# The last turns of a two-layer graph attention kernel: an order of their own, and late steps on other engines

## The chip, the cores and the metric

The kernel runs on one core of one Trainium2 chip. The metric is the device time of one execution in microseconds (us). It was taken in three runs: 3034.12, 3035.43 and 3037.57 us, with a median of 3035.43 us. One further execution was recorded by the hardware profiler, and all times of single instructions come from it.

The engines are named as the profile names them. PE is the matrix engine and PEld its loading of weights. DVE is the vector engine, ACT the scalar (activation) engine, POOL the GpSimd engine, and SP the engine that issues the transfers. Each engine works through its own instructions in the order in which the program issues them.

## What is computed

There are 128 graphs of 128 nodes with 512 features, and an adjacency matrix for each. Two layers follow each other, each of the form `x = x + layer(relu(layernorm(x)))`.

```python
# layer 0, 8 heads of 64
m = embs @ map_w.T + map_b
n = sem / norm                              # m, split into heads, at unit length
cos_adj = (n @ n.T masked) > 0.1
p_attn = softmax(q @ k.T / 8, masked) * keep
adj = cos_adj * p_attn
out = relu(((adj @ sem_h) @ gcn_W.T) / (adj.sum(-1) + 1))
# layer 1, 4 heads of 64
attn = softmax(q @ k.T / 8, masked by adjacency)
return x + ((attn @ v) @ Wo + bo)
```

All is in float32.

## The kernel before

**Blocks and turns.** The 128 graphs are cut into 64 blocks of two graphs (`g` = 0 and 1, each 128 nodes on the 128 partitions). A block is an object of the class `Block` (L224); each of its methods is one *step*, which issues a few instructions. The tuple `TURN` (L910) lists 139 entries `(back, step, arguments)`. The loop at L1155 runs turns from -2 to 67. In a turn it goes through the list and runs each step for block `turn - back`, if there is such a block. So a block is spread over some eight turns: loading at back -3, projections of layer 0 at back 0, its attention at back 1, the end of layer 0 and the projections of layer 1 at back 2, the scores of layer 1 at back 3, and the output at back 4. The order of each engine's instructions is the order of this list. It is written out by hand (`tc.manual_schedule()`, L1071), and the list is the same for all turns. In the last turns 63 to 67 the steps of blocks that don't exist drop out, and the rest stays in the order of `TURN`.

**The steps of a block**, in the order of its life, with the engine that does the work:

- `p qk i`, `p ms i` (L378, PE): the seven products of a 2x2 Strassen scheme for queries and keys, and for `m` with the layer's second map. The banks are called X, Y and Z. `r`, `u`, `c` (L442 to L493, DVE, ACT, POOL) combine and drain them. Product 7 adds to bank Y after `u 1` has read it, product 4 after `u 2`, product 3 adds to Z after `c 1 1`.
- `squares` (ACT), `norms` (DVE), `unit` (L511, POOL): rows of `m` at unit length. For a block in the middle, 32x32 pieces are then transposed on the DVE and moved through DRAM: `nT`, `nT_put`, `nT_get`, `nT_out`. The first and the last block are `alone` (L230); for them PE transposes (L543) and ACT copies.
- `scores0` (PE), `scores0_out`, `max0` (DVE), `exps0` (ACT); `near` (PE), `near_out` (L632, DVE): scores, softmax numerators, and the cosine test. `near_T`, `near_put`, `near_get`, `near_T_out`: the transpose of this tile through DRAM, or by PE for a block that is `alone`.
- `mix0` (PE), `mix0_out` (L702, DVE), `residual` (L722, POOL), `stats1` (DVE), `rstd` (L329, POOL), `norm1` (ACT): layer 0 ends and layer 1 begins.
- `h1`, `h1_put`, `h1_get`, `h1_out` (L736 to L757): the transpose of the normed rows, through DRAM, or by PE for the last two blocks (`late`, L228). `halves` (L360, POOL): four sums of quarters for the Strassen products.
- `p qk1`, `p v` (PE) with their `r`, `u`, `c`; `scores1` (PE), `scores1_out` (L775, DVE), `exps1` (L808, ACT), `weights1` (L820, DVE, one reciprocal), `scale1` (L824, POOL, two instructions).
- `attn_T` (DVE), `attn_put`, `attn_get` (SP, four writes and a read): the transpose of the weights through DRAM. For the last block alone (`last`, L229) PE transposes and ACT copies (L855 to L863).
- `mix1` (PE), `mix1_out` (L881, ACT), `project` (L886, PE), `project_out` (L899, DVE), `store` (L904, SP). `bias1` (L732, POOL) adds the output bias to the residual beforehand.

**What is shared.** All PSUM tiles come from one pool of eight banks (L58 to L61), which are given out in turn: a product that asks for a bank waits until the readers of the bank handed out eight requests earlier are done. Most tiles in SBUF have one buffer (`keep1`), so a block's step waits for the previous block's last reader. `x1`, the residual rows, has three buffers and is loaded by `reload` (L249).

Of the kernel before, what the change touches and what calls it, by code (L numbers as in the profile page):

```python
# [10 lines left out]
AF = mybir.ActivationFunctionType  # L11
ALU = mybir.AluOpType
# [3 lines left out]
P = 128  # L16
# [4 lines left out]
def kernel(  # L21
# [21 lines left out]
    nc = tc.nc  # L43
    B, S, D = x.shape
# [6 lines left out]
    IC = INNER // P  # L51
    G = 2
    T = G * S
    NB = B // G
# [128 lines left out]
    squares = ctx.enter_context(tc.tile_pool(name="squares", bufs=2))  # L183
# [40 lines left out]
    class Block:  # L224
        def __init__(self, b):
            self.b = b

            self.late = b >= NB - 2  # L228
            self.last = b == NB - 1  # L229
            self.alone = b == 0 or self.last  # L230
            self.f = {}

        def cols(self, g):
# [125 lines left out]

        def halves(self, layer):  # L360
            A = self.quarters(layer)
            tag = f"halves{layer}"
            t = keep1.tile([P, 4, 2, S], F32, tag=tag, name=f"{tag}_{self.b}")
            S1, S2, S3, S4 = (t[:, i] for i in range(4))
            nc.gpsimd.tensor_tensor(S1, A[1][0], A[1][1], ALU.add)  # L365
            nc.gpsimd.tensor_tensor(S2, S1, A[0][0], ALU.subtract)
            nc.gpsimd.tensor_tensor(S3, A[0][0], A[1][0], ALU.subtract)
            nc.gpsimd.tensor_tensor(S4, A[0][1], S2, ALU.subtract)
            self.f["S", layer] = (S1, S2, S3, S4)

        def parts(self, kind, nm):
# [6 lines left out]
        def p(self, kind, i):  # L378
            layer = int(kind in ("qk1", "v"))
            A = self.quarters(layer)  # L380
            S = self.f.get(("S", layer))
# [339 lines left out]

        def residual(self, g):  # L722
            x1 = self.x1[:, g, :]
            nc.gpsimd.tensor_add(x1, x1, self.f["mix", g])  # L724

        def stats1(self, g):
            self.f["st", 1, g] = stats(self.x1[:, g, :], f"1_{self.b}_{g}")
# [32 lines left out]

        def scores1(self):
            f = self.f
            f["ps1"] = self.by_square(f"ps1_{self.b}", "c q" if self.last else "q c")
            for g in range(G):
                cols = self.cols(g)
                self.pairs(
                    f["ps1"],
                    g,
                    lambda r, p: f["q1"][r, p, cols],
                    lambda r, p: f["k1"][r, p, cols],  # L770
                    IC,
                    G,
                )

        def scores1_out(self):  # L775
            b, f = self.b, self.f
            pp = f["ps1"]
            if self.last:
                flat = keep1.tile([P, 2, IC, G, Q, SQ], F32, tag="s1", name=f"s1_{b}")
                f["s1_flat"] = flat  # L780
                s = flat.rearrange("p r c g q j -> p q r c g j")
            else:
                s = keep1.tile([P, Q, 2, IC, G, SQ], F32, tag="s1", name=f"s1_{b}")
            mx = small.tile([P, 2, IC, G], F32, tag="mx1", bufs=2, name=f"mx1_{b}")
            neg = self.neg1.rearrange("p q g j -> p q (g j)")
            for par in range(2):
                if self.last:
                    for c in range(IC):
                        nc.vector.tensor_add(  # L789
                            s[:, :, par, c].rearrange("p q g j -> p g q j"),  # L790
                            pp[par][:, :, c * G : (c + 1) * G].rearrange("p q g j -> p g q j"),
                            self.neg1.rearrange("p q g j -> p g q j"),
                        )
                    row = flat[:, par].rearrange("p c g q j -> p (c g) q j")
                else:
                    nc.vector.tensor_add(
                        s[:, :, par].rearrange("p q c g j -> p q c (g j)"),
                        pp[par].rearrange("p q (c g) j -> p q c (g j)", g=G),
                        neg[:, :, None, :].broadcast_to([P, Q, IC, G * SQ]),
                    )  # L800
                    row = s[:, :, par].rearrange("p q c g j -> p (c g) q j")
                nc.vector.tensor_reduce(  # L802
                    mx[:, par].rearrange("p c g -> p (c g)"), row, AX.XY, ALU.max, negate=True
                )
            f["s1"], f["mx1"] = s, mx
            f["z1"] = small.tile([P, 2, IC, G], F32, tag="z1", bufs=2, name=f"z1_{b}")

        def exps1(self, g):  # L808
            s, mx, z = (self.f[k] for k in ("s1", "mx1", "z1"))
            for par in range(2):  # L810
                for c in range(IC):
                    nc.scalar.activation(  # L812
                        s[:, :, par, c, g, :],
                        s[:, :, par, c, g, :],
                        AF.Exp,
                        bias=mx[:, par, c, g : g + 1],
                        accum_out=z[:, par, c, g : g + 1],
                    )

        def weights1(self):  # L820
            s, z = self.f["s1"], self.f["z1"]
            nc.vector.reciprocal(z, z)  # L822

        def scale1(self):  # L824
            s, z = self.f["s1"], self.f["z1"]
            for par in range(2):
                if self.last:
                    t = self.f["s1_flat"][:, par].rearrange("p c g q j -> p (c g) (q j)")
                    zz = z[:, par].rearrange("p c g -> p (c g)")[:, :, None]
                    nc.gpsimd.tensor_tensor(t, t, zz.broadcast_to([P, IC * G, S]), ALU.mult)  # L830
                    continue
                nc.gpsimd.tensor_tensor(  # L832
                    s[:, :, par].rearrange("p q c g j -> p q (c g) j"),
                    s[:, :, par].rearrange("p q c g j -> p q (c g) j"),
                    z[:, par].rearrange("p c g -> p (c g)")[:, None, :, None].broadcast_to(
                        [P, Q, IC * G, SQ]
                    ),
                    ALU.mult,
                )

        def attn_T(self):
            if self.last:
                return
            s = self.f["s1"].rearrange("p q r c g j -> p (q r c g j)")
            nc.vector.transpose(s, s)

        def attn_put(self):
            if self.last:
                return
            s = self.f["s1"].rearrange("p q r c g j -> p q (r c g j)")  # L850
            self.f["attn_dram"] = put(s, "attn", f"attn_{self.b}")

        def attn_get(self):
            t = keep1.tile([P, Q, 2 * IC * G * SQ], F32, tag="aT", name=f"aT_{self.b}")
            if self.last:  # L855
                src = self.f["s1_flat"].rearrange("p r c g q j -> p (r c g q j)")
                t = self.flat(t)
                for i, pi in enumerate(self.transposes(src, 2 * IC * G)):
                    nc.scalar.copy(t[:, i * D : (i + 1) * D], pi)
                self.f["aT"] = t.rearrange(  # L860
                    "p (r c g a j) -> p a r c g j", r=2, c=IC, g=G, j=SQ
                )
                return  # L863
            get(self.f["attn_dram"], t)
            self.f["aT"] = t.rearrange("p a (r c g j) -> p a r c g j", r=2, c=IC, g=G)
# [14 lines left out]

        def mix1_out(self):  # L881
            oT = keep1.tile([P, G, IC, S], F32, tag="oT", name=f"oT_{self.b}")
            nc.scalar.copy(oT, self.f["po1"])  # L883
            self.f["oT"] = oT

        def project(self, g):  # L886
# [23 lines left out]
    TURN = (  # L910
        (2, "mix0", 0),
        (4, "mix1"),
        (2, "mix0", 1),
        (2, "mix0_out", 0),
        (2, "residual", 0),
        (1, "scores0", 0),
        (4, "mix1_out"),
        (1, "nT_put"),
# [130 lines left out]
        (1, "near_T_out", 1),  # L1049
    )  # L1050

    blocks = {}

    def block(b):
# [16 lines left out]
    with tc.manual_schedule():  # L1071
# [12 lines left out]
        for i in range(2):  # L1084
            t = keep3.tile([P, G, D], F32, tag="x1", name=f"wT_k{i}")
# [9 lines left out]
        t = keep1.tile([P, G, KC, S], F32, tag="h1T", name="gw0")  # L1095
        gw.append(t.rearrange("p g c s -> p (g c s)"))
        t = keep1.tile([P, Q, 2, IC, G, SQ], F32, tag="s1", name="gw1")
# [53 lines left out]
        halves = (-1, "halves", 0)  # L1151
        early = [t for t in TURN if t != halves]
        early.insert(early.index((0, "unit", 0)), halves)

        for turn in range(1 + min(t[0] for t in TURN), NB + 4):  # L1155
            for back, step, *args in early if turn < 2 else TURN:
                b = turn - back
                if 0 <= b < NB and (b, step, *args) not in done:
                    getattr(block(b), step)(*args)
                    if later and turn >= 0 and step in ("u", "c") and args[0] == "ms":  # L1160
                        one_piece()
            blocks.pop(turn - 4, None)


# [44 lines left out]
```

## Time and profile before

| | |
|---|---|
| median of three runs | 3035.43 us |
| the profiled execution, its own time | 3033.84 us |
| its span, from the first to the last instruction | 3032.0 us |
| mean granted clock of PE | 0.996 |
| PE busy | 2990.2 us (99%) |
| DVE busy | 2410.0 us (79%) |
| POOL busy | 1768.7 us (58%) |
| ACT busy | 1471.3 us (49%) |
| one turn in the middle (PE's `mix1` of one turn to that of the next) | 45.7 us |

The profiled execution took 1.84 us more than its span, and 1.6 us less than the median of the three runs. A turn is read off the timeline of PE: the products of `mix1` start at 2621.59, 2667.30 and 2713.01 us. The stretch of 45.7 us from 2711.5 us on has PE busy in all of it, with DVE at 37.5, POOL at 27.6 and ACT at 22.8 us.

Turn 63, the last in which a block runs its projections of layer 0, starts on PE at 2894.85 us with `mix0` of block 61. A line of the timeline has the start, the duration, the engine, the line of the kernel, what is written and read, how many instructions are merged, and in brackets how long the engine was idle before and which instruction ended that.

### The profile page before, as it was taken

To read this page: it belongs to the slowest core of one execution; us is meant where nothing else is said; L and a number is where in the kernel's file an instruction comes from. 1 tells how busy PE (TensorE), PEld (TensorE's weight loads), DVE (VectorE), ACT (ScalarE), POOL (GpSimd) and SP (SyncE) were. 2 spreads that over 40 slices of the span, in tenths; PEclk is the share of its full clock that TensorE was granted. 3 is DMA by queue.
4 is the path that set the end of the run, shared out by engine and by line. 5 is a ranking of instruction groups with operands and counts; after the bars stand their busy time and mean duration, and the time that the engine had idled before them with its cause. 6 is when DMAs were issued, how large, how long until landed. Compare 5 with 4: busy or idle time off the path is not lost. (4 is left out here: it accounts for less than half of the span.)

```text
span 3032.0 us, 68538 instructions
## 1 busy us (share of the span) xinstructions
PE 2990.2 (99%) x25328; PEld 2372.9 (78%) x25328; DVE 2410.0 (79%) x4563; ACT 1471.3 (49%) x4637; POOL 1768.7 (58%) x2439
## 2 busy tenths in 40 slices
PE   8999999999999999999999999999999999999996
PEld 5788788787787787787787787787787787787775
DVE  3788888888888888888888888888888888888873
ACT  2454454554554554554554554554554554544542
POOL 1566566566566566566566566566565565565552
PEclk9999999999999999999999999999999999999998
DMA  4356556555556555565565565565465465465441
GB/s 155 109 159 185 175 166 182 171 172 182 166 177 182 160 183 182 156 188 177 156 191 177 156 188 182 152 191 181 149 194 179 149 192 181 149 189 181 147 140 56
DMA packets 304830, 508.39 MB, mean 168 GB/s; under 512 B 49264, under 2 KB 181104, under 8 KB 296560
## 3 DMA queue, kind: packets, MB, share of 16 engines
q1 hardware_dynamic: 301792, 503.44, 54.5%
q8 instruction: 201, 3.29, 0.4%
q10 hardware_dynamic: 2704, 0.57, 0.1%
q14 instruction: 133, 1.09, 0.1%
HBM read 273.72 MB, written 230.16 MB: 166 GB/s over the span
## 5 line engine op out<-in xcount | busy, mean ns | idle before, releaser
L617 ACT ACTIVATE s<-s,mx 128x128 f32<-128x128 f32 x1024 | 396.3, 393 | 74.1 <-DVE mx L603 74.1
L513 POOL TENSOR_TENSOR rn<-rn,mhalf 128x8 f32<-128x8 f32 x128 | 213.1, 1665 | 330.6 <-DVE rn L508 258.5
L407 PEld LDWEIGHTS py_qk<-halves,w_qk 128*128 128x128 f32 x3072 | 370.4, 193 | 41.4 <-issue 31.8
L407 PE MATMUL py_qk<-halves,w_qk 128*128 128x128 f32 x3072 | 389.2, 277 | 10.5 <-DVE k L476 6.7
L407 PEld LDWEIGHTS pz_qk<-halves,w_qk 128*128 128x128 f32 x3072 | 369.0, 192 | 28.7 <-issue 28.7
L407 PE MATMUL pz_qk<-halves,w_qk 128*128 128x128 f32 x3072 | 385.7, 275 | 0.0
L407 PEld LDWEIGHTS px_qk<-hT,w_qk 128*128 128x128 f32 x2048 | 244.0, 192 | 39.9 <-issue 32.4
L365 POOL TENSOR_TENSOR halves<-h1T 128x256 f32<-128x256 f32 x64 | 46.6, 728 | 387.9 <-ACT h1T L319 381.0
L812 ACT ACTIVATE s<-s,mx 128x128 f32<-128x128 f32 x512 | 199.2, 390 | 142.7 <-DVE mx L802 142.7
L407 PE MATMUL px_qk<-hT,w_qk 128*128 128x128 f32 x2048 | 256.8, 279 | 3.5 <-DVE mix L713 3.5
L395 PE MATMUL px_ms<-w_ms,hT 128*128 128x512 f32 x512 | 247.2, 605 | 0.0
L890 PE MATMUL py<-w_o,oT 128*128 128x512 f32 x512 | 240.7, 594 | 1.4 <-ACT oT L883 1.4
L395 PE MATMUL py_ms<-w_ms,halves 128*128 128x512 f32 x512 | 240.7, 592 | 0.0
L395 PE MATMUL pz_ms<-w_ms,halves 128*128 128x512 f32 x512 | 240.6, 592 | 0.0
L319 ACT ACTIVATE hT<-mv 128x1024 f32<-128x1024 f32 x64 | 67.6, 1057 | 318.1 <-PE py_ms L395 318.1
L724 POOL TENSOR_TENSOR x<-x,mix 128x512 f32<-128x512 f32 x128 | 162.6, 1271 | 89.5 <-DVE mix L713 57.3
L456 ACT ACTIVATE r_qk<-px_qk,b_k 128x128 f32<-128x128 f32 x256 | 73.2, 368 | 275.6 <-PE px_qk L407 271.2
L617 ACT ACTIVATION_READ_ACCUMULATOR s<-s,mx 128x1 f32 x1024 | 196.6, 192 | 0.0
L395 PEld LDWEIGHTS pz_ms<-w_ms,halves 128*128 128x128 f32 x512 | 97.3, 190 | 122.5 <-issue 107.6
L832 POOL TENSOR_TENSOR s<-s,z 128x512 f32<-128x512 f32 x126 | 128.5, 1041 | 106.0 <-DVE z L822 106.0
L395 PEld LDWEIGHTS px_ms<-w_ms,hT 128*128 128x128 f32 x512 | 92.0, 189 | 99.5 <-issue 91.8
L641 DVE SCALAR_TENSOR_TENSOR s<-pc,s 128x512 f32<-128x512 f32 x256 | 163.6, 680 | 3.3 <-PE pc L557 3.1
(140 smaller groups left out, 7121.8 us busy)
## 6 DMA issues: line engine op xcount, KB each, us to landing
d_h<-hn SPq DMA_DIRECT2D x504, 128.0 KB, 3.7
mv<-d_h SPq DMA_DIRECT2D x126, 512.0 KB, 4.4
d_near<-s SPq DMA_DIRECT2D x248, 256.0 KB, 3.8
near_mv<-d_near SPq DMA_DIRECT2D x62, 1024.0 KB, 5.4
xt<-in_x SPq DMA_DIRECT2D x64, 512.0 KB, 7.3
x<-in_x SPq DMA_DIRECT2D x64, 512.0 KB, 6.3
out<-x SPq DMA_DIRECT2D x128, 256.0 KB, 2.3
d_attn<-s SPq DMA_DIRECT2D x252, 128.0 KB, 2.4
```

The costliest lines, as they stand in the source:

```text
L319: nc.scalar.activation(t.rearrange("p g c (a j) -> p (g c) a j", a=Q), self.f.pop((key, "moved")).rearrange("p a r j -> p r a j"), func,)
L365: nc.gpsimd.tensor_tensor(S1, A[1][0], A[1][1], ALU.add)
L395: nc.tensor.matmul(bank[:, : rhs.shape[1]], lhsT=src[:, c, :], rhs=rhs, start=(first and c == 0), stop=(c == 1), skip_group_check=True,)
L407: nc.tensor.matmul(bank[:, oc * P : (oc + 1) * P], lhsT=(w_qk1 if layer else w_qk)[:, w, c, oc * P : (oc + 1) * P], rhs=src[:, c, :], star ...
L456: nc.scalar.activation(r[:, cols], X[:, cols], AF.Identity, bias=b_k[:, oc : oc + 1])
L513: nc.gpsimd.tensor_tensor(rn, rn, mhalf[:, :H0], ALU.pow)
L617: nc.scalar.activation(s[:, :, g, par, c, :], s[:, :, g, par, c, :], AF.Exp, bias=mx[:, i : i + 1], accum_out=z[:, h : h + 1],)
L641: nc.vector.scalar_tensor_tensor(sp, cp, 0.1, sp, ALU.is_gt, ALU.mult,)
L724: nc.gpsimd.tensor_add(x1, x1, self.f["mix", g])
L812: nc.scalar.activation(s[:, :, par, c, g, :], s[:, :, par, c, g, :], AF.Exp, bias=mx[:, par, c, g : g + 1], accum_out=z[:, par, c, g : g + 1],
L832: nc.gpsimd.tensor_tensor(s[:, :, par].rearrange("p q c g j -> p q (c g) j"), s[:, :, par].rearrange("p q c g j -> p q (c g) j"), z[:, par ...
L890: nc.tensor.matmul(py, lhsT=self.f["oT"][:, g, c, :], rhs=w_o1[:, c, :], start=(c == 0), stop=(c == IC - 1),)
```

## The change

A second list, `TAIL`, takes the place of turns 63 to 67. In it `back` counts from 64, so that 1 is block 63, 2 is block 62, and so on to 5 for block 59. It holds the same steps as `TURN` gives for these turns; left out are only steps that do nothing for the last blocks. Their order is new, and it isn't one turn after another: the products of blocks 61, 62 and 63 are mixed.

For the two `late` blocks (62 and 63) some steps change engine or form:

- `residual` and `halves` of layer 1 go from POOL to DVE.
- Block 62 gets what only block 63 had: rows of scores in the order that PE can transpose, eight transposes on PE, and no way through DRAM for the attention.
- `exps1` takes one parity of heads instead of one graph, and scales it at once: four exponentials on ACT, then a reciprocal and one multiplication on DVE. `weights1` and `scale1` are empty for these blocks.
- Of the two copies of the transposed attention the second goes to DVE; `mix1_out` is split into a half on ACT and a half on DVE.

```diff
-            self.last = b == NB - 1
-            self.alone = b == 0 or self.last
+            self.alone = b == 0 or b == NB - 1
...
+            add = (nc.vector if self.late and layer else nc.gpsimd).tensor_tensor
...
+            add(S1, A[1][0], A[1][1], ALU.add)
+            add(S2, S1, A[0][0], ALU.subtract)
+            add(S3, A[0][0], A[1][0], ALU.subtract)
+            add(S4, A[0][1], S2, ALU.subtract)
...
-            nc.gpsimd.tensor_add(x1, x1, self.f["mix", g])
+            (nc.vector if self.late else nc.gpsimd).tensor_add(x1, x1, self.f["mix", g])
...
-            f["ps1"] = self.by_square(f"ps1_{self.b}", "c q" if self.last else "q c")
+            f["ps1"] = self.by_square(f"ps1_{self.b}", "c q" if self.late else "q c")
...
+        def exps_last(self, par):
+            s, mx, z = (self.f[k] for k in ("s1_flat", "mx1", "z1"))
+            for c in range(IC):
+                for g in range(G):
+                    nc.scalar.activation(
+                        s[:, par, c, g],
+                        s[:, par, c, g],
+                        AF.Exp,
+                        bias=mx[:, par, c, g : g + 1],
+                        accum_out=z[:, par, c, g : g + 1],
+                    )
+            nc.vector.reciprocal(z[:, par], z[:, par])
+            t = s[:, par].rearrange("p c g q j -> p (c g) (q j)")
+            zz = z[:, par].rearrange("p c g -> p (c g)")[:, :, None]
+            nc.vector.tensor_tensor(t, t, zz.broadcast_to([P, IC * G, S]), ALU.mult)
...
-                    nc.scalar.copy(t[:, i * D : (i + 1) * D], pi)
+                    copy = nc.vector.tensor_copy if i else nc.scalar.copy
+                    copy(t[:, i * D : (i + 1) * D], pi)
...
-            nc.scalar.copy(oT, self.f["po1"])
+            if self.late:
+                nc.scalar.copy(oT[:, 0], self.f["po1"][:, 0])
+                nc.vector.tensor_copy(oT[:, 1], self.f["po1"][:, 1])
+            else:
+                nc.scalar.copy(oT, self.f["po1"])
...
-        for turn in range(1 + min(t[0] for t in TURN), NB + 4):
+        for turn in range(1 + min(t[0] for t in TURN), NB - 1):
...
+        for back, step, *args in TAIL:
+            getattr(block(NB - back), step)(*args)
```

The new list, with its entries written side by side and cut to the parts that the prediction speaks of (a number is `back`):

```text
3 mix0 0, 3 mix0 1, 3 mix0_out 0, 5 mix1, 3 residual 0, 2 scores0 1, 3 mix0_out 1, 3 stats1 0, 3 residual 1
...
2 max0 1, 5 store 0, 3 norm1 1, 3 h1, 2 exps0 0 0, 1 p qk 5, 1 c qk 0 0, 3 h1_put
...
1 p qk 3, 3 h1_get, 1 r qk 2, 2 near_out 0, 2 near_out 1, 3 h1_out, 1 p ms 1, 1 p ms 6, 3 halves 1,
1 c qk 1 0, 1 c qk 0 1, 1 p ms 5, 3 p v 1, 2 near_T 0, 2 near_T 1
...
2 mix0 0, 3 c v 1 1, 4 attn_put, 2 mix0_out 0, 3 p v 3, 3 c v 0 1, 2 mix0 1, 1 unit 1, 2 residual 0,
2 mix0_out 1, 1 scores0 0, 2 stats1 0, 2 residual 1, 2 stats1 1, 2 rstd 1 0, 2 rstd 1 1, 2 norm1 0,
4 attn_get, 1 nT_out, 1 scores0_out 0, 2 norm1 1, 1 scores0 1, 4 mix1, 4 mix1_out, 3 scores1, 1 max0 0,
1 scores0_out 1, 1 exps0 0 0, 2 h1_out, 1 near 0, 3 scores1_out, 4 project 1, 4 project_out 1, 4 project 0,
1 exps0 0 1, 3 exps1 0, 1 near_out 0, 3 exps1 1, 2 halves 1, 1 near_T_out 0, 4 project_out 0, 1 near 1
...
3 scale1, 1 reload, 3 attn_T, 2 r qk1 1, 2 p qk1 2, 3 attn_put, 2 u qk1 1, 2 p v 7
...
2 p v 3, 1 mix0 1, 2 c qk1 0 1, 1 residual 0, 3 attn_get, 3 mix1, 1 stats1 0, 2 c v 0 1, 1 mix0_out 1,
3 mix1_out, 1 residual 1, 1 rstd 1 0, 1 stats1 1, 1 norm1 0, 2 scores1, 3 project 1, 3 project_out 1,
1 rstd 1 1, 1 norm1 1, 1 bias1 1, 3 project 0, 2 scores1_out, 1 h1_out, 1 halves 1, 3 store 1,
1 p qk1 1, 1 r qk1 1, 1 p qk1 5, 1 p v 6, 1 p qk1 6, 3 project_out 0, 1 u qk1 1, 2 exps1 0, 1 p v 1, 1 p qk1 7
...
2 bias1 1, 1 c qk1 1 0, 1 u v 2, 1 p qk1 3, 1 p v 4, 2 exps1 1, 1 c v 1 0, 1 p v 5, 1 c qk1 0 1, 1 c qk1 0 0,
2 attn_get, 1 masks1, 1 scores1, 1 scores1_out, 2 mix1, 2 mix1_out, 2 bias1 0, 1 p v 2, 1 c v 1 1, 2 project 0,
1 exps1 0, 1 p v 3, 2 project_out 0, 2 store 0, 1 c v 0 0, 1 c v 0 1, 1 exps1 1, 2 project 1, 1 attn_get,
3 store 0, 1 mix1, 2 project_out 1, 2 store 1, 1 mix1_out, 1 project 1, 1 bias1 0, 1 project 0,
1 project_out 1, 1 store 1, 1 project_out 0, 1 store 0
```

## The prediction

> **What bounds the kernel now.** I read the page first. PE is 99% busy and its row is at 9 in all but the first and the last slice, so only what shortens PE's row counts, and only the tail is changed.
>
> ```profile
> PE   8999999999999999999999999999999999999996
> ...
> PEclk9999999999999999999999999999999999999998
> ```
>
> The last slice has both faults: PE not full, and its clock lowered. The table of windows from turn 63 to the end shows where (columns: us, busy us and instructions of each engine, granted PE clock, DMA share, GB/s).
>
> ```profile
> core 0: us, PE busy (x) PEld busy (x) DVE busy (x) ACT busy (x) POOL busy (x), PEclk, DMA share, GB/s
> 2895.00:2940.50 45.50, 45.50 (x392) 36.27 (x390) 34.92 (x66) 20.03 (x69) 25.25 (x32) 1.00 0.47 140
> 2940.50:2963.00 22.50, 18.54 (x210) 15.08 (x208) 16.61 (x36) 15.20 (x59) 10.84 (x16) 0.92 0.06 24
> 2963.00:2985.00 22.00, 18.90 (x180) 16.30 (x180) 10.15 (x29) 3.42 (x8) 6.40 (x10) 0.84 0.26 72
> 2985.00:3005.00 20.00, 13.86 (x108) 12.96 (x108) 7.98 (x17) 6.79 (x24) 9.56 (x13) 0.91 0.26 81
> 3005.00:3032.00 27.00, 13.44 (x62) 7.13 (x57) 5.47 (x11) 5.64 (x20) 2.04 (x2) 0.83 0.10 39
> ```
>
> Turn 63 is full. From 2940.56 us on PE waits. Its timeline has nine waits, 21.70 us together; these four are 17.42 of them:
>
> ```profile
> 2954.60 2.08 PE L557 MATMUL pc<-nT 64*128 64x128 f32 x16 [3.49 <-ACT nT L547]
> ...
> 2966.09 2.05 PE L407 MATMUL py_qk<-halves,w_qk 128*128 128x128 f32 x8 [3.44 <-DVE k L476]
> ...
> 2995.49 2.04 PE L407 MATMUL py_qk<-halves,w_qk 128*128 128x128 f32 x8 [3.29 <-DVE k L476]
> ...
> 3017.93 2.12 PE L297 MATMUL pt<-ident,s 128*128 128x128 f32 x8 [7.20 <-POOL s L830]
> ```
>
> The group behind each takes double time: eight `py_qk` products need 0.89 us elsewhere and 1.84 here (to the next group's start), with a granted clock of 0.50 in two-microsecond windows. Against full-clock groups the excess is 1.7 us behind the first, 2.7, 1.7 and 2.9 behind the others: 9.0 us. So from PE's start of turn 63 (2894.85, t = 0 below) to the span's end, 137.15 us are: 45.7 of turn 63, 55.9 of products after it (64.9 busy less 9.0), 21.7 waiting, 9.0 slow clock, and 4.85 behind the last product (3027.15 to 3032.0).
>
> The chain of waits tells why. `k` L476 (`u qk1 1`) stands on DVE behind `attn_T`, which waits for `scale1` on POOL:
>
> ```profile
> 2991.43 0.21 DVE z L822
> 2991.65 0.07 issue
> 2991.71 2.05 POOL s L832 x2
> 2993.79 0.04 DVE s L845
> ```
>
> **Part by part.**
>
> *PE's own work.* 45.7 + 55.9 = 101.6 us stay; eight transposes for block 62 are added, 0.97 us by nT's (2948.98 to 2949.95): 102.6.
>
> *Block 62's attention.* Gone: a DVE transpose (1.25), four writes and a read on SP. From 2993.79 to the read's landing (issue 2998.85 plus the tail's median of 4.2) that way took 9.3 us; SP has nothing else queued behind it. In its place are the transposes, a 0.59 ACT copy and a DVE copy of 0.68 (PSUM source, as L902). `scores1_out` has four additions of 0.41 for two of 0.69: +0.2 on a DVE that idles half of that stretch.
>
> *Scaling.* POOL's pair is 2.04 us. DVE with both inputs in SBUF takes 0.68 for 128x512 (the weight subtractions of L1148): two of those and two reciprocals of 0.2, and the first overlaps the other parity's exponentials. For block 63 that takes about 1.2 us off the chain.
>
> *Halves, residuals.* Eight POOL instructions of 0.73 become DVE instructions of 0.41 (L1148, 128x256); four of 1.27 become 0.68. DVE gets some 8.7 us with the scaling, POOL loses 15. DVE had 40 us of work in the 91 after turn 63, so there is room on average, not everywhere: at t = 42 to 68 I find it busy throughout.
>
> *Split copy of mix1_out.* 0.59 on ACT becomes two concurrent halves of about 0.4: 0.2 us each for blocks 62 and 63.
>
> *The order.* I walked the new list by hand, each engine in order at the durations of the rows above, with bank and tile reuse. PE stays full through t = 48.9. The DRAM round trips moved into it still fit: h1 of block 61 is transposed at 16.4 (11.7 before), lands near 25 and its relu ends at 26, needed at 29.2; near of block 62 lands by 42, needed at 45.2. Then the waits, without contention / with it:
>
> 1. Transposes of block 63's `n`: PE is free at 48.9; `unit` ends on POOL at 50.0 (two powers of 1.65, four products of 0.6, from `norms` at 44): 1.2 / 1.9.
> 2. `scores1` 61 needs the bank that `scores0_out` 63 frees; DVE gets there after two `mix0_out` (1.65 each), residuals (0.68), `stats1` (0.93): 0.9 / 1.2.
> 3. `h1_out` 62, whose `norm1` stands behind nT's copies on ACT: 0.6 / 0.6.
> 4. `near_T_out` 63 waits for four exponentials of 0.38, relus of 1.2, four more, and `near_out`: 1.1 / 1.1.
> 5. `p v 3` and `mix0 1`: 0.4 / 0.4.
> 6. Block 63's products wait for its `halves`: 0.3 / 3.8.
> 7. The end: `scores1` 63 now has 5.3 us of other products behind it, `mix1` and `project` of 62 and two `p v`, against a chain of about 6. With the copies of aT (0.9) and oT (0.6): 2.2 / 2.2.
>
> Sum 6.7 / 11.2. `attn_put` 61 now follows `reload` 63 on SP, which waits for block 60's stores and moves 512 KB: 0 to 2 us, I take 1. `nT_put`, `near_put` and the other transfers keep their neighbours.
>
> *The contention* is where a rule speaks against this change. The row first: POOL's first `halves` takes 0.73 us, but 1.39 where DVE ran subtractions with two SBUF inputs (L175); a small DVE instruction of 0.23 took 0.58 and ended with POOL's.
>
> ```profile
> 45.56 1.39 POOL L365 TENSOR_TENSOR halves<-hT 128x256 f32<-128x256 f32 x1 [12.63 <-ACT hT L319]
> ```
>
> ```profile
> 2944.01 0.58 DVE L710 TENSOR_SCALAR r<-r,free 128x8 f32<-128x8 f32 x1
> ```
>
> The Trainium skill ("SBUF — State Buffer", section "SBUF: two separate sides") says that DVE and GpSimd share one pair of ports as an exclusive lock, taken by a DVE instruction with two SBUF inputs for its whole length. All 16 moved instructions have two. At `halves` 63 POOL is about to run three `bias1` (1.27 each) and `masks1` (2 x 0.69) in a row, and each DVE half can wait for one of them: 1.3 + 0.7 + 0.7 + 1.3, less overlap, 3.5. Without the rule I would take 6.7 us of waits, by it 11.2; the rows say it holds, and I take 10 because POOL need not win each time.
>
> *The clock.* "TensorE: Matmul & The Clock Gate", "What's actually happening", puts the drop after an idle window of about 3.4 us; here 3.29 was enough, while 0.74, 0.66 and 1.46 between 2984.9 and 2990.2 left it at 1.00. By either, none of the waits above (1.9 at most in one piece) costs clock: 0, bounded by 2.7 for one drop.
>
> *The last store.* Before, both additions and both stores followed the last product: 4.85. Now only one of each does: 0.69 + 0.41 issue + 2.3 landing + 0.45 = 3.9.
>
> **Sum.** 102.6 + 11 + 0 + 3.9 = 117.5 against 137.15: 19.6 us less. The span becomes 3012.4, that execution 3014.2; the median stood 1.6 above it: 3016 us.
>
> **Rivals.** *Contention or a late chain is worse than taken*: one or two waits of 3 us open again, each with 1.7 to 2.9 us of half clock: 5 to 12 us back, 3021 to 3028. For it: DVE full from 42 to 68, where every delay passes on; against: 91 us of tail with three half-idle engines. *No contention*: 6.7 + 0 waits, 24 us gained, 3011. *The order does nothing*, since block 63's chain sets the end anyway: within 6 us of 3035. Against: PE would need 25 us of waits, and block 63's `mix0` in the walk is at 71, where before it came at 82.5. *Slower*: the order breaks the full turn 63. h1 61 is 3.3 us from being late, near 62 about 3, attention 60 and 61 under 1. PE can't pass a late product, so each trip late beyond this costs its lateness plus about 2.5 of clock. To lose the 19.6 us and 6 more, the four must be some 6 us late each, trips of 14 in place of 8. The trace's put-to-landing times (medians in the tail: 2.3 to 4.1 us for writes, 3.1 to 5.4 for reads) are far from that.
>
> **Numbers.** Forecast as summed, 0.58 (3012 to 3020); no contention 0.12; worse contention 0.21; nothing 0.05; slower 0.04. A measurement can tell about 0.2% (6 us) from no change. Faster by over 0.2%: 0.91; within: 0.05; slower: 0.04. For 8 in 10 I leave out the far half of the second rival's gains and the last two cases: 3009 to 3025.
>
> **What would show it.** After 2940 us the clock row stays at 1.00; PE's waits in the tail sum to about 11 us and none exceeds 2.5; DVE `halves` at 0.41, those of block 63 stretched or spaced by POOL's `bias1`; PE waits before `pt` of the last attention under 1 us. Wrong: a PE wait over 3 us before `py_qk` of block 63 or before `mix1` of 61, or any wait before t = 48.

## The result and the profile after

The changed kernel takes 3009.97 us (median of five runs, 3009.67 to 3010.41) against 3035.43 us before (five runs, 3033.86 to 3037.57): 25.5 us less. The ratio is 0.9915, with a 95% interval of 0.9904 to 0.9926. The forecast was 3016 us with a range of 3009 to 3025; the result is 6.0 us below it, just inside the lower end. The profiled execution took 3010.06 us with a span of 3008.3. That span is only 23.7 us shorter, because turn 63 began 1.3 us later in this execution (2896.14 in place of 2894.85 us), a shift that is there from the first turns on and that the change doesn't touch.

The rows of PE and of its clock, from the page of the changed kernel:

```profile
PE   8999999999999999999999999999999999999999
...
PEclk9999999999999999999999999999999999999999
```

The last slice is now full and at full clock. The table of windows shows the same for the tail (the columns are those of the table of the kernel before):

```profile
2940.50:2963.00 22.50, 21.42 (x240) 17.28 (x240) 20.29 (x48) 14.41 (x52) 11.08 (x16) 1.00 0.23 71
2963.00:2985.00 22.00, 21.24 (x215) 17.81 (x214) 17.27 (x45) 10.14 (x36) 10.28 (x14) 1.00 0.25 85
2985.00:3005.00 20.00, 18.18 (x126) 12.40 (x124) 12.50 (x30) 6.37 (x26) 0.00 (x0) 1.00 0.14 52
```

DVE, the third busy column, is busier than before in the same stretches, and the clock is 1.00 in all of them. PE's timeline lists five waits after turn 63 where it listed nine:

```profile
2950.58 1.16 PE L557 MATMUL ps<-k,q 64*128 64x128 f32 x14 [0.97 <-ACT nT L547]
...
2979.44 1.16 PE L407 MATMUL px_qk<-h1T,w_qk 128*128 128x128 f32 x8 [0.25 <-ACT h1T L753]
2980.97 1.13 PE L407 MATMUL pz_qk<-halves,w_qk 128*128 128x128 f32 x8 [0.37 <-DVE halves L365]
...
2998.24 1.63 PE L892 MATMUL po<-aT,v 128*64 128x128 f32 x16 [0.24 <-ACT aT L879]
3000.80 3.70 PE L914 MATMUL py<-w_o,oT 128*128 128x512 f32 x8 [0.92 <-DVE oT L905]
```

They sum to 2.75 us, where before it was 21.70, and no group behind them runs at double length. So the account of the tail, from PE's start of turn 63 to the span's end, is 137.15 us before and 112.16 after (3008.3 - 2896.14): waits 18.95 less, half clock 9.0 less, the piece behind the last product 1.05 less (4.85 to 3.8), the eight new transposes 0.97 more. That would be 28.0 us; 25.0 were measured, and 3.0 us lie inside the rows of PE's products.

A part of these 3.0 us is waiting too. A row merges several products, and a wait in the middle of it doesn't show in its bracket, but it does in the rows of PEld, which loads the weights:

```profile
2946.42 0.42 PEld L296 LDWEIGHTS pt<-ident,n 128*128 128x128 f32 x4 [0.35 <-POOL n L523]
...
2984.03 0.97 PEld L407 LDWEIGHTS py_qk<-halves,w_qk 128*128 128x128 f32 x8 [0.33 <-DVE k L476]
2994.70 0.52 PEld L395 LDWEIGHTS pz_v<-w_v,halves 128*128 128x128 f32 x4 [0.88 <-DVE v L482]
2998.79 0.85 PEld L892 LDWEIGHTS po<-aT,v 128*64 128x64 f32 x14 [0.35 <-DVE aT L879]
```

By the starts of the groups around them, these four cost PE some 0.4, 0.3, 0.3 and 0.5 us, 1.5 together; the kernel before has one such wait at full clock, of 0.4 (before product 6 of block 62). So about 1.1 of the 3.0 us are waits, and 1.9 are in PE's work proper.

### The profile page after: what moved, and what is told of

The parts are those of the page before. It is cut to its first block, busy times and chain, and to the rows that moved or that the text cites. A ratio compares the mean times of both kernels' runs of the same rounds, so it can differ in the third digit from the quotient of the medians.

```text
span 3008.3 us, 68541 instructions
## 1 busy us (share of the span) xinstructions
PE 2986.0 (99%) x25336; PEld 2367.4 (79%) x25336; DVE 2418.2 (80%) x4586; ACT 1469.3 (49%) x4637; POOL 1750.9 (58%) x2423
## 3 DMA queue, kind: packets, MB, share of 16 engines
q8 instruction: 201, 3.29, 0.4%
## 4 chain that ended last, share of the span: by engine, by line
PE 97%; DVE 1%; DMA 1%; POOL 0%; issue 0%; ACT 0%; ACTq 0%; SPq 0%; DVEq 0%; POOLq 0%
PE py_qk L407 17%; PE px_qk L407 11%; PE pz_qk L407 11%; PE py_ms L395 11%; PE px_ms L395 8%; PE pz_ms L395 7%; PE py L914 7%; PE po L692 4%; PE psc L557 4%; PE pc L557 4%; PE py_v L395 3%; PE ps L557 2%; PE pz_v L395 2%; PE px_v L395 2%; PE po L892 2%; PE pw_k L132 0%
## 5 line engine op out<-in xcount | busy, mean ns | idle before, releaser
L617 ACT ACTIVATE s<-s,mx 128x128 f32<-128x128 f32 x1024 | 396.4, 393 | 73.0 <-DVE mx L603 73.0
L815 ACT ACTIVATE s<-s,mx 128x128 f32<-128x128 f32 x496 | 192.9, 390 | 136.2 <-DVE mx L802 136.2
L395 PEld LDWEIGHTS py_ms<-w_ms,halves 128*128 128x128 f32 x512 | 92.5, 190 | 92.8 <-issue 92.5
```

What stands on the lines that cost most here:

```text
L395: nc.tensor.matmul(bank[:, : rhs.shape[1]], lhsT=src[:, c, :], rhs=rhs, start=(first and c == 0), stop=(c == 1), skip_group_check=True,)
L617: nc.scalar.activation(s[:, :, g, par, c, :], s[:, :, g, par, c, :], AF.Exp, bias=mx[:, i : i + 1], accum_out=z[:, h : h + 1],)
L815: nc.scalar.activation(s[:, :, par, c, g, :], s[:, :, par, c, g, :], AF.Exp, bias=mx[:, par, c, g : g + 1], accum_out=z[:, par, c, g : g + 1],
```

## The experiments

All are compared with their own runs of the kernel before (medians 3035.03, 3035.55 and 3034.48 us in the three sets), and by their medians with the 3009.97 us of the changed kernel. That was timed in a set of its own (3035.43 us before), and the medians of the kernel before differ by up to 1.1 us between the sets: a smaller difference from the changed kernel is not shown.

**The moves in the old order.** Theory: the new order carries the gain. Rival: the moves of steps to other engines carry it.

```diff
-        for turn in range(1 + min(t[0] for t in TURN), NB - 1):
+        for turn in range(1 + min(t[0] for t in TURN), NB + 4):
...
-        for back, step, *args in TAIL:
-            getattr(block(NB - back), step)(*args)
```

> All engine and form changes of the late blocks, but the last turns in the old order of TURN. Theory (the order carries the gain): near 3030 us, a gain of 3 to 8 us. The way through DRAM of block 62's attention is gone (3.3 us of wait and 1.7 of clock), the last scaling is some 1.2 us shorter, but in the old order the vector engine now stands behind block 62's exponentials before it comes to block 63's halves, which gives 2 to 3 us back. The waits before near of block 63 (3.5) and before block 62's Strassen product 7 (3.4) stay. Rival (the moves carry it): 3018 us or less, with PE waits below 10 us in the tail.

Measured: 3035.44 us, ratio 1.0001 (0.9992 to 1.0010). The moves alone gain nothing, less than either side expected. PE's timeline of this kernel still has ten waits with 20.06 us, and three of the four largest have new releasers:

```profile
2956.49 2.08 PE L557 MATMUL pc<-nT 64*128 64x128 f32 x16 [4.20 <-ACT nT L547]
2966.02 2.04 PE L407 MATMUL py_qk<-halves,w_qk 128*128 128x128 f32 x8 [2.78 <-DVE halves L366]
...
2995.40 1.68 PE L407 MATMUL py_qk<-halves,w_qk 128*128 128x128 f32 x8 [4.60 <-DVE halves L366]
...
3017.98 1.09 PE L296 MATMUL pt<-ident,s 128*128 128x128 f32 x4 [4.38 <-DVE s L838]
```

The 3.29 us behind `attn_T` of block 62 are gone, as the removal of that transpose must do, and the 7.20 us at the end are 4.38 and 0.45. But the halves, now on DVE, stand behind a reciprocal that waits for the exponentials on ACT, and PE waits for the halves 4.60 us where it had waited 1.46.

**The same, with the halves left on POOL.** This tests that reading.

```diff
-            add = (nc.vector if self.late and layer else nc.gpsimd).tensor_tensor
+            add = nc.gpsimd.tensor_tensor
```

> Old order of the last turns, all engine and form changes except that the halves stay on POOL. Theory: the moves alone gained nothing because block 62's and 63's halves then stand on DVE behind instructions that wait for the exponentials (PE waits of 2.78 and 4.60 us before Strassen product 6). With the halves on POOL these waits fall below 2 us and the kernel is 3 to 7 us faster than before, 3028 to 3032 us. Rival (the old order takes the gain elsewhere, in the product 7 behind the reciprocals and scaling): within 2 us of before, 3033 to 3037 us.

Measured: 3032.56 us, ratio 0.9989 (0.9980 to 0.9997), 2.9 us faster than the moves with the halves on DVE. The wait for block 63's halves is 1.46 us again; block 62's product 7 still waits for `u` on DVE, 2.80 us in place of 3.44. So the place of the halves costs the old order about 3 us, and the rest of the moves is worth about 3 us there, just under the theory's range.

**The order alone.** The new list, with every step on its old engine and block 62's attention through DRAM. The steps of that way got places in the list (only this part of the edit is shown, with entries side by side).

```diff
+        (2, "exps1", 1), (2, "weights1"), (2, "scale1")
...
+        (2, "attn_T"), (2, "attn_put")
...
         (2, "attn_get")
```

> The new order with everything else as before: halves, residuals and scaling on POOL, copies on ACT, block 62's attention through DRAM (its transpose behind the second u of v, its scaling and writes beside it, since the new order has no working place for them). Theory: 12 to 18 us faster than before, 3017 to 3023 us; it keeps the closed waits before near of block 63 and the end, and opens one of 4 to 6 us before mix1 of block 62, with half clock behind it. Rival (the moves carry it): 3027 us or more.

Measured: 3018.14 us, ratio 0.9946 (0.9931 to 0.9961). 16.9 us of the 25 come from the order alone, within the theory's range. One long wait is left, and it is the one that was expected:

```profile
2991.10 1.16 PE L558 MATMUL ps<-k,q 64*128 64x128 f32 x16 [0.85 <-DVE k L483]
2997.60 1.98 PE L892 MATMUL po<-aT,v 128*64 128x128 f32 x16 [5.34 <-DMA aT<-d_attn]
```

DVE shows a second price of that way, on the same transfer: the writes to DRAM read the scores' single buffer, and block 63's scores can't be written until they have landed.

```profile
2994.45 0.75 DVE L790 TENSOR_TENSOR s<-ps,neg 128x256 f32<-128x256 f32 x2 [3.50 <-DMA d_attn<-s]
```

**Only block 62's attention back through DRAM**, all else as changed. Its steps stand where the run with the order alone has them.

> The changed kernel with only block 62's attention back on its way through DRAM (POOL scaling, DVE transpose, four writes and a read, placed as in the run with the order alone); halves, residuals and block 63 as changed. Theory (the order needs this one form change, the other moves are small): 5 to 7.5 us slower than the changed kernel, 3015 to 3017.5 us, with a PE wait of 4 to 6 us before mix1 of block 62 and half clock behind it. Rival (the small moves add up to the difference of 8 us between the order alone and the whole change): 3012 us or less.

Measured: 3017.81 us, ratio 0.9941 (0.9925 to 0.9958), 7.8 us slower than the changed kernel and 0.3 us above the range that I gave it. The wait before `mix1` of block 62 is 5.18 us and the groups behind it run long (1.98 us for one that takes 1.09). This one move makes up nearly all of the 8.2 us between the order alone and the whole change.

**Halves and residuals on POOL in the new order.**

```diff
-            add = (nc.vector if self.late and layer else nc.gpsimd).tensor_tensor
+            add = nc.gpsimd.tensor_tensor
...
-            (nc.vector if self.late else nc.gpsimd).tensor_add(x1, x1, self.f["mix", g])
+            nc.gpsimd.tensor_add(x1, x1, self.f["mix", g])
```

> The changed kernel with halves and residuals of the late blocks back on POOL; all else as changed. Theory: eight instructions of 0.73 in place of 0.42 and four of 1.27 in place of 0.68, on the path of block 62 and 63: 2 to 4 us slower than the changed kernel, 3012 to 3014 us. By the contention as the prediction counted it (3.5 us at the halves of block 63, more at the residuals), the way back would cost nothing or win: 3008 to 3011 us.

Measured: 3011.55 us (3011.27 to 3011.65), ratio 0.9922 (0.9908 to 0.9937). It is 1.6 us slower by the medians, a little more than the sets differ among themselves, and no run of it is as fast as any run of the changed kernel. That is a little under the theory's 2 to 4, and against the contention term.

**Scaling on POOL in the new order.**

```diff
-            nc.vector.tensor_tensor(t, t, zz.broadcast_to([P, IC * G, S]), ALU.mult)
+            nc.gpsimd.tensor_tensor(t, t, zz.broadcast_to([P, IC * G, S]), ALU.mult)
```

> The changed kernel with only the scaling of the late blocks' attention on POOL, one instruction of about 1.03 us per parity in place of 0.69 on DVE. Theory: it is on the path once, at the last parity of block 63: 0.5 to 1.5 us slower than the changed kernel, 3010.5 to 3011.5 us. If scaling is what closed the 7.2 us wait, several us slower, with a PE wait of 2 us or more before the last transposes.

Measured: 3010.10 us, ratio 0.9918 (0.9902 to 0.9935): no difference from the changed kernel. The scaling's engine is not what closed the wait at the end: with it on POOL, PE's timeline lists no wait before the last transposes.

**No late `bias1`.** It takes away the POOL work that the prediction set against block 63's halves; the output bias of the last four graphs is missing.

```diff
         def bias1(self, g):
+            if self.late:
+                return
```

> The changed kernel without bias1 for blocks 62 and 63: the output bias of the last four graphs is left out. It takes away the POOL instructions that the prediction put beside block 63's halves (three of 1.27 us). By the prediction's contention term, 2 to 3.5 us faster than the changed kernel: 3006.5 to 3008 us. Theory from the trace (the first half waited 0.3 us, the scaling of block 62 0.5): 0 to 0.6 us faster, 3009.4 to 3010 us.

Measured: 3010.69 us (3009.93 to 3011.10), ratio 0.9917 (0.9903 to 0.9932). It is not faster. The first of block 63's halves went from 0.74 to 0.42 us, block 62's first scaling from 1.15 to 0.69, and PE's wait for the halves vanished, but PE waited 0.75 us for block 61's attention from DRAM in this run, a wait that the changed kernel's profile doesn't list. The contention term of 3.5 us is refuted; what is left of it is below 1 us.

**The two engines side by side.** A test appended behind the last store: 12 DVE additions of two SBUF tiles beside six POOL instructions of three kinds.

```diff
+        meet(0); dve(6)
...
+        for kind in ("tt", "u8", "f32"):
+            pool(kind, 4)
+        for k, kind in enumerate(("tt", "u8", "f32")):
+            meet(k + 1)
+            dve(12)
+            pool(kind, 6)
```

> The changed kernel with a test appended behind its last store; its total time isn't compared, only the instructions of the test are read. DVE additions of two SBUF tiles (128x512) run alone, then beside POOL additions of two tiles (128x512), beside POOL comparisons with one uint8 input (128x256), and beside POOL additions of a constant with one float input (128x512). By the exclusive lock as the prediction took it, DVE's 0.68 us goes to about 1.3 to 2 us, and POOL's instructions lengthen, in all three. By what the changed kernel's trace suggests (the halves of block 63 beside masks1 took 0.43), only the two-input POOL instructions hold DVE up; beside the one-input ones DVE stays at 0.65 to 0.75 and POOL alone is longer.

DVE's timeline has the six additions alone first, then twelve beside each kind of POOL instruction (the column behind the start is the time of the whole row):

```profile
3009.23 3.69 DVE L1507 TENSOR_TENSOR xw<-xu 128x512 f32<-128x512 f32 x6
...
3028.80 13.69 DVE L1507 TENSOR_TENSOR xw<-xu 128x512 f32<-128x512 f32 x12
...
3042.73 8.30 DVE L1507 TENSOR_TENSOR xw<-xu 128x512 f32<-128x512 f32 x12
...
3052.07 9.37 DVE L1507 TENSOR_TENSOR xw<-xu 128x512 f32<-128x512 f32 x12
```

POOL's, four of each kind alone and then six of each beside DVE:

```profile
3013.17 4.92 POOL L1515 TENSOR_TENSOR xo<-xa 128x512 f32<-128x512 f32 x4
3018.18 4.56 POOL L1517 TENSOR_SCALAR xo<-xe 128x256 f32<-128x256 uint8 x4
3022.82 5.88 POOL L1519 TENSOR_SCALAR xo<-xa 128x512 f32<-128x512 f32 x4
...
3029.53 10.01 POOL L1515 TENSOR_TENSOR xo<-xa 128x512 f32<-128x512 f32 x6
...
3043.57 8.39 POOL L1517 TENSOR_SCALAR xo<-xe 128x256 f32<-128x256 uint8 x6
...
3052.91 9.87 POOL L1519 TENSOR_SCALAR xo<-xa 128x512 f32<-128x512 f32 x6
```

A DVE addition alone takes 0.62 us (3.69 / 6). The row of twelve beside POOL's two-input additions averages 1.14, but that mixes two kinds: POOL's six were over after 10.0 us, and only six of the twelve were held up by them. One by one in the trace, these took about 1.74 us each, with 1.66 from start to start, and the others 0.68. POOL's six took 1.67 each in place of 1.23. Six of both need 3.7 + 7.4 = 11.1 us one after the other; side by side they took 10.0, so they do nearly exclude each other. The twelve beside the uint8 comparison average 0.69, those beside the one-input float addition 0.78, and here both rows run beside POOL's for almost their whole length, while POOL's own go from 1.14 to 1.40 and from 1.47 to 1.65. The exclusion holds between two-input instructions; with one input on POOL it is a loss of 12% to 27% on either engine. In the run with the moves in the old order it can be seen in the kernel itself: two halves beside `scale1`, a two-input instruction.

```profile
2964.49 2.29 POOL L851 TENSOR_TENSOR s<-s,z 128x512 f32<-128x512 f32 x2 [10.46 <-DVE z L844]
2964.73 1.14 DVE L366 TENSOR_TENSOR halves<-halves,h1T 128x256 f32<-128x256 f32 x1
2965.80 1.25 DVE L367 TENSOR_TENSOR halves<-h1T 128x256 f32<-128x256 f32 x1
```

**The end of the list in the old order.** The new list up to `attn_get` of block 62; what follows is sorted as `TURN` has it.

```diff
+        cut = TAIL.index((2, "attn_get"))
...
+        end = sorted(TAIL[cut:], key=lambda t: rank[t])
+        for back, step, *args in TAIL[:cut] + tuple(end):
```

> The changed kernel with the new list up to attn_get of block 62, and what follows in the order of TURN: the last products of block 63's v, mix1 and project of block 62 come before scores1 of block 63 instead of behind it. Theory: the chain from the last scores to the last transposes, about 6 us, lies open again: a PE wait of 4 to 5.5 us before the last transposes, with up to 3 us of half clock, 5 to 8 us slower than the changed kernel, 3015 to 3018 us. If the end's gain came from the faster scaling, less than 2 us slower.

Measured: 3022.95 us, ratio 0.9962 (0.9947 to 0.9977), 13.0 us slower than the changed kernel, more than the 5 to 8 expected. The wait that I had named is there, with the size that I gave it; the rest is its neighbours.

```profile
2994.71 3.70 PE L914 MATMUL py<-w_o,oT 128*128 128x512 f32 x8 [0.93 <-DVE oT L905]
...
3004.01 1.09 PE L296 MATMUL pt<-ident,s 128*128 128x128 f32 x4 [4.51 <-DVE s L838]
3005.55 1.08 PE L296 MATMUL pt<-ident,s 128*128 128x128 f32 x4 [0.46 <-DVE s L838]
...
3010.37 5.42 PE L914 MATMUL py<-w_o,oT 128*128 128x512 f32 x8 [0.98 <-DVE oT L905]
```

Block 62's `project` loses the cover of its copy (0.93), the transposes come in two pieces, the last `project` is 1.7 us longer at half clock, and both stores are at the very end again (5.1 us behind the last product in place of 3.8).

**The copy of `mix1_out` whole on ACT.**

```diff
-            if self.late:
-                nc.scalar.copy(oT[:, 0], self.f["po1"][:, 0])
-                nc.vector.tensor_copy(oT[:, 1], self.f["po1"][:, 1])
-            else:
-                nc.scalar.copy(oT, self.f["po1"])
+            nc.scalar.copy(oT, self.f["po1"])
```

> The changed kernel with mix1_out whole on ACT for the late blocks too (0.59 us, no DVE half). As the prediction had it (two halves at once, 0.2 us saved for each block): 0.2 to 0.4 us slower. If the halves run one after the other (0.37 + 0.42): PE's wait before the last project goes from 0.92 to about 0.73 and the time stays or falls by 0.2 us; either is below what can be measured, so PE's wait decides.

Measured: 3010.10 us, ratio 0.9920 (0.9903 to 0.9936), no difference. PE's wait before the last `project` falls from 0.92 to 0.73 us. The split saves nothing.

**Two swaps in the list.**

```diff
-        (2, "norm1", 0),
         (4, "attn_get"),
         (1, "nT_out"),
+        (2, "norm1", 0),
...
-        (1, "project", 1),
-        (1, "bias1", 0),
         (1, "project", 0),
+        (1, "bias1", 0),
+        (1, "project", 1),
```

> The changed kernel with two small swaps in the new list: for block 63 project 0 goes before project 1 (with its additions and stores), so that PE begins on the half copied by ACT, and nT_out of block 63 goes before norm1 of block 62, so that ACT's copies don't stand behind a wait for POOL. Theory: the split copy runs one half after the other (the DVE half started when the ACT half had ended), so the first swap saves 0.4 us, the second 0 to 0.5: 3009.0 to 3009.6 us, at the edge of what five rounds can tell. If the wait is for something else, no difference.

Measured: 3009.51 us (3008.98 to 3009.85), ratio 0.9917 (0.9903 to 0.9932). By the medians that is 0.46 us faster than the changed kernel, but the two were not timed in the same set and their runs overlap, so it isn't shown. The waits went as expected: 0.46 in place of 0.92 before the last `project`, and the 0.97 before `scores1` became 0.57 before `h1_out`. It is the lowest median of all.

## Why the prediction was right, and where it was off

The direction and the mechanism held: the long waits and the half clock behind them went, and that is the gain. The time is inside the range by 1.0 us only. Of the prediction's cases, "no contention" (24 us gained, 3011) is the nearest, but its number is luck in part: the waits came out shorter than its 6.7 us and PE's own work longer, and the two errors offset each other.

- **The four long waits close.** Right, and it is the order that closes most: 16.9 us with the order alone. The run with the old end shows that 13 of the 25 us hang on the last part of the list. The prediction gave the whole sum and didn't say which part would carry it; alone, the moves are worth 0, or 3 us with the halves left on POOL.
- **Block 62's attention.** The prediction told its 9.3 us way but put no price on it for the path. It is 7.8 us in the new order. In the old order the same change stood in kernels that gained 0 and 3 us, so its worth depends on the order.
- **Scaling, residuals, halves.** The prediction had "about 1.2 us off the chain" for block 63's scaling: 0.1 measured, which is not told apart from nothing. Halves and residuals are worth 1.6 us. The split copy was to save 0.2 us a block: nothing.
- **The waits, items 1 to 7.** Taken as 10 of 6.7 to 11.2; the profile lists 2.75, and with those inside the rows it is some 4.3.
  - Item 6 failed most: 0.3 or 3.8, measured 0.37. It took every POOL instruction as a lock; but the two `masks1` instructions beside the halves have one input, and DVE's second and third half took 0.43 and 0.42 beside them, while of the `bias1` two were nearly done (POOL 2978.05 to 2980.55) when the first half came at 2980.09. Contention did stretch an instruction that the prediction did not charge: block 62's first scaling, 1.15 us beside a `bias1`.
  - Item 1 (1.2) cost 0.4. The transposes of the first graph need only the first `unit`; I had let all eight wait for the second. Item 4 (1.1) isn't there at all, for the same reason: the transposes of block 63's `near` began at 2957.31, before `near_out`'s second half had ended (2957.68). Items 3 and 5 aren't listed either.
  - Item 2 had the right size (0.97 for 0.9 to 1.2) and not the right cause: the trace names ACT's copy of `nT` as the releaser and not DVE's `scores0_out`, and the run with two swaps, which puts these copies ahead of `norm1`, is rid of this wait. In the two runs with halves and residuals on POOL in the new order it is `scores0_out` (1.00). The hit is luck.
  - Item 7 (2.2) was nearly right: 0.24 and 0.92 listed, and inside the rows some 0.3 before `p v 3` and 0.5 for the second copy of aT, 2.0 together. The 0.3 us before product 7 of block 63 are in no item.
- **`reload` ahead of `attn_put`, 0 to 2 us, taken as 1.** None in the changed kernel; in four of the other runs PE waits 0.26 to 0.75 us for the read of block 61's attention. It is the next thing to become late; whether `reload` delays it wasn't tried.
- **The clock.** Right: no drop. The runs that reopen a wait of 4.2 us or more have long groups behind it again, and a shorter one did it too: in the two runs with the moves in the old order the granted clock fell from 1.00 to 0.50 behind waits of 2.78 and 2.80 us. So the 3.29 us of the prediction's rows is not the shortest that costs clock. The longest that left it at 1.00 is 1.46 us; the lengths between were not met.
- **The last store.** 3.9 forecast, 3.8 measured.
- **PE's own work.** 102.6 forecast; 108.36 from the start of turn 63 to the last product, less 2.75, is 105.6, and about 1.1 of the 3.0 us between them are the waits inside rows. The prediction put nothing on the other 1.9. Cutting groups apart has a price: `scores0` of two graphs in a row takes 1.99 us, while alone between other products one takes 1.09 (2944.56 to 2945.65), 0.19 more for two. But the new list does little more of it: the timeline has 91 rows of products in the tail in place of 89, and the form of the weights (such as 64*128 or 128*64) changes 29 times between neighbours in place of 21. At 0.1 us a change, an estimate from `scores0`'s figures, that is under 1 us; the rest is open, and no run tests it.

So the terms that were mis-sized are the waits (11 with the 1 us for `reload`, in place of 2.75 listed) and, the other way, PE's products with the waits inside their rows (3.0 too little). The first is larger, and the difference is the 5.3 us by which the tail came out shorter than 117.5.

What stays open besides: the price of the old end (13 us) is named part by part from its timeline, not taken apart by runs.

## What to carry to other kernels

At the end of a pipelined kernel the steady-state order has nothing left to put behind the last chain; give the tail its own order in which another block's products stand between a score and its transpose, before moving work between engines. Then look at what that order leaves waiting: here it was one trip through DRAM, and taking it away gave the next 7.8 us. Moving a step to a faster engine is worth only what its new neighbours in the queue leave: on DVE the same halves were 3 us worse behind a waiting reciprocal, and 1.6 us better together with the residuals in a list that put them elsewhere. When walking a list by hand, let each product wait only for the part of the tile that it reads, look for waits in the rows of PEld as well as PE, and check the number of SBUF inputs on both engines before charging a lock.

## What the runs showed of the hardware

- DVE and POOL exclude each other almost fully where both have two SBUF inputs (1.74 us for a DVE addition that alone takes 0.62 to 0.68), but hardly where POOL has one (0.69 and 0.78 on average). The rule that the prediction cited makes no such distinction, and the measurement decides.
- A copy split between ACT and DVE, both from one PSUM bank into one tile, ran one half after the other: DVE's half waited 0.99 us and was released by ACT's. The copies of aT, from two banks, overlapped. Whether the bank or the program's own waits make the difference wasn't tried.

```profile
2997.61 0.59 ACT L879 COPY aT<-pt 128x512 f32<-128x512 f32 x1 [1.43 <-PE pt L296]
2998.04 0.69 DVE L879 COPY aT<-pt 128x512 f32<-128x512 f32 x1 [0.93 <-PE pt L296]
...
2999.91 0.37 ACT L904 COPY oT<-po 128x256 f32<-128x256 f32 x1 [1.72 <-PE po L892]
3000.32 0.42 DVE L905 COPY oT<-po 128x256 f32<-128x256 f32 x1 [0.99 <-ACT oT L904]
```

- PE's clock: behind waits of 2.78 us and more the granted clock fell to 0.50 for some microseconds; single waits of 1.46 us and less that began at 1.00 left it there.
